# A conv-attention-MoE layer on one core: routing laced into the attention-only steps, with a new step order

## The chip, the core and the metric

The kernel runs on one core of a Trainium2 chip. Five engines work side by side, each through its own list of instructions in order: PE (TensorE, matrix products into PSUM), DVE (VectorE), ACT (ScalarE, functions from tables that must be loaded), POOL (GpSimd) and SP (SyncE, which here only starts DMA transfers). ACT and POOL start transfers too. Engines wait for each other by semaphores. The metric is the device time of one execution in microseconds (us); lower is better.

## The reference

`x` is 16 images of 128 channels and 64 x 64 pixels, thus 4096 tokens each. In float32:

```python
x = x + mamba(group_norm(x))           # state-space scan over tokens, 16 states, 256 inner channels
t = tokens(x)
t = t + causal_attn(layer_norm(t))     # 8 heads, one query vector each; prefix softmax over tokens
t = t + moe(layer_norm(t))
# moe, per image of 4096 tokens:
logits = n @ gate_w.T + gate_b         # 64 experts
probs  = softmax(logits, axis=tokens)
vals, idx = top_k(probs, 8)            # every expert takes its 8 best tokens
pooled = sum_k n[idx] * vals           # one row of 128 per expert
out = gelu(pooled @ w1 + b1) @ w2 + b2
result[token] += out[expert] * vals    # for the tokens that the expert took
```

## The kernel before

**Joint steps.** Every image is cut into 8 blocks of 512 tokens, so there are 128 blocks and the main loop makes one step for each. The scan (mamba) works on block k and the attention on block k - 9. A step has 16 parts n, one for each state. In each, DVE makes a product `bx` (`product`) and two scans of 512 (`scan`); POOL multiplies the result by the broadcast C row (`da`) and PE adds it up into `y_ps`; SP loads the next states' B and C rows as a broadcast from memory (`load_bc`, three n ahead, five buffers); ACT makes the decays (`decay`, an Exp, up to eight n ahead). For n = 1, 3, 5 and 7 a POOL transfer adds a pair of products instead (`add_pair`).

**The order by hand.** All other work is placed by the table `STEP`: for each n three strings, one before the first scan, one between the two scans and one after them. A name in it is an operation: `k0`..`k7` keys, `s0 s1` scores, `v0`..`v7` values, `mx less sexp` score maximum and exponential, `w0 w1` weights from the split scores, `a..` attention products, `d` one decay, `y..` a transpose-add of one state, `lnsc lnap` layer norm, `ge0`..`ge4` the end of the group norm, `ar0`..`ar3` the residual added to a finished image by POOL transfers with addition, `sr0`..`sr3` its store, `spread` the reading back of the split scores, `tu fin` the turn and store of half an attention block. All engines keep this order, and SP, ACT and POOL their transfers in it.

**Attention-only steps.** After the 128th block the scan is over. The loop goes on for ten more steps with the attention's last nine blocks (the tenth is short). DVE and POOL have almost nothing to do there.

**Routing.** A loop of its own follows. A pair of images is handled together (8 pairs, 64 blocks). For every block it loads the channel columns `t` of both images, turns them on PE (`turn`), takes mean and variance on DVE (8 `bn_stats`, 8 `bn_aggr`), makes logits (16 PE records), scales and turns them, normalizes the tokens on ACT (`normed`, 8 activations). Once per pair `choose` finds the 8 largest logits of every expert among 4096, takes Exp and keeps the chosen ones; twelve blocks later `turn_chosen` and `pool_chosen` sum the tokens.

**Experts and final sum.** 16 groups of 4 experts with weights in four buffers, then for every image a product of outputs and chosen probabilities added to `t2_d` and stored.

PSUM is shared by small pools: `ps` has three banks that nearly all PE results pass through.

Of the kernel before, what the change touches and what calls it, by code (L numbers as in the profile page):

```python
# [11 lines left out]
ALU = mybir.AluOpType  # L12
# [27 lines left out]
def conv_attn_hybrid(ctx: ExitStack, tc: tile.TileContext, x, w_in, conv_w, conv_b, w_xproj, w_dt, b_dt,  # L40
# [27 lines left out]
    g_d = dram.tile([NB // 2, P, T], F32, name="g_d")  # L68
    o_d = dram.tile([NB, E, O], F32, name="o_d")
# [4 lines left out]
    ones = const.tile([P, P], F32, name="ones")  # L74
    nc.gpsimd.memset(ones, 1.0)
# [6 lines left out]
    with ExitStack() as st:  # L82
# [3 lines left out]
        yps = st.enter_context(tc.tile_pool(name="yps", bufs=1, space=PSUM))  # L86
        bps = st.enter_context(tc.tile_pool(name="bps", bufs=1, space=PSUM))
# [26 lines left out]
        wv = wp.tile([P, HD, P], F32, name="wv")  # L114

# [100 lines left out]

        xp = st.enter_context(tc.tile_pool(name="xp", bufs=1))
        xsp = st.enter_context(tc.tile_pool(name="xsp", bufs=2))
        xbp = st.enter_context(tc.tile_pool(name="xbp", bufs=2))
        mp = st.enter_context(tc.tile_pool(name="mp", bufs=2))  # L220
        m1 = st.enter_context(tc.tile_pool(name="m1", bufs=1))
        dap = st.enter_context(tc.tile_pool(name="dap", bufs=13))
        hp_ = st.enter_context(tc.tile_pool(name="hp", bufs=2))
        bcp = st.enter_context(tc.tile_pool(name="bcp", bufs=5))
        tmp = st.enter_context(tc.tile_pool(name="tmp", bufs=6))
        vp_ = st.enter_context(tc.tile_pool(name="vp", bufs=4))
        a1 = st.enter_context(tc.tile_pool(name="a1", bufs=1))
# [30 lines left out]
        def gn_end(b, part):  # L258
# [11 lines left out]
            if part == 2:  # L270
                DVE.tensor_tensor(gs[:, 1:2], mv[:, 0:1], gs[:, 0:1], ALU.subtract)
                DVE.scalar_tensor_tensor(gs[:, 1:2], gs[:, 1:2], gs[:, 1:2], mv[:, 1:2], ALU.mult, ALU.add)
# [191 lines left out]
        def store_residual(b, part):  # L464
            SP.dma_start(t1_d[b, :, bass.ts(part, T // 4)], res[b][:, bass.ts(part, T // 4)])
# [236 lines left out]
        def take_o(m):  # L702
            s = att[m]
            s["ot"] = short("ot")
            ACT.copy(s["ot"][:, : 2 * P], s.pop("o")[:, :2, :].rearrange("p q d -> p (q d)"))

        def turn_o(m, f):
            s = att[m]
            s["to"] = bank("to_ps")
            ot = s.pop("ot")  # L710
            for q in range(2):
                PE.transpose(s["to"][:, bass.ts(q, P)], ot[:, bass.ts(q, P)], ident)

        def finish(m, f):
            b, i = divmod(m, NBLK)
            s = att[m] if f == 0 else att.pop(m)
            xs = short("tx")
            ACT.copy(xs[:, : 2 * P], s.pop("to")[:, : 2 * P])
            ACT.dma_start(t2_d[b, :, i * L + f * (L // 2) : i * L + (f + 1) * (L // 2)], xs[:, : 2 * P])

# [4 lines left out]
            ("lx0 k0 k4 yp14", "yp15", "takey k1 k2"),  # L725
            ("k3 v6", "norm skip", "tu0 fin0"),
            ("", "k5", "ge0 s0 k6 turny ge1 k7"),
            ("s1", "gate0", ""),
            ("v4 v7 ge2 gate1 v5 mx d d y-1 conv0", "d less y1", "sexp"),
            ("w1 a10 a11 exp d ts1", "ge3 outp d put tsc ssp c1 d", ""),  # L730
            ("", "", "conv1"),
            ("ar0 ssum ar1 b1 d slog rest1 ar2 split1 y3 to1 rest2 d conv2 csilu", "split2", "d store v0"),
            ("tu1 lx1 v2 ge4", "fin1 cen", ""),
            ("", "", ""),
            ("v1 xproj v3 z delta sq exp bcs", "var", "lnsc"),
            ("", "y5 y7", "spread inv w0 d"),
            ("gnl a00 a01", "y8", "d y9 lb ar3 sr0"),
            ("sr1 d y10 y11 ts0 d", "c0 y12", ""),
            ("b0", "", "sr2"),
            ("d lnap gns", "du", "nt d d sr3 y13 d d to0"),  # L740
# [37 lines left out]

        for k in range(NK + LAG + 1):
            b, i = divmod(k, NBLK)  # L780
            cur = k if k < NK else None
# [37 lines left out]
            for f in range(2):  # L819
                ops[f"tu{f}"] = (mp_, lambda m, f=f: turn_o(m, f))  # L820
                ops[f"fin{f}"] = (mp_, lambda m, f=f: finish(m, f))
# [9 lines left out]
            def do(n, part):  # L831
                for name in STEP[n][part].split():
                    if name == "d":
                        decays(k, n, 1)
                        continue
                    of, f = ops[name]
                    if of is not None:
                        f(of)

# [19 lines left out]
    ff = ctx.enter_context(tc.tile_pool(name="ff", bufs=1))  # L859
    pooled = ff.tile([P, E, 32], F32, name="pooled")  # L860
    nc.gpsimd.memset(pooled, 0.0)
    with ExitStack() as st:
        PE, DVE, ACT, POOL, SP = (InOrder(tc, e) for e in (nc.tensor, nc.vector, nc.scalar, nc.gpsimd, nc.sync))
        NG = CB * 2
        LATE = 12
        AHEAD = 5
        xps = st.enter_context(tc.tile_pool(name="rxps", bufs=2, space=PSUM))
        lps = st.enter_context(tc.tile_pool(name="rlps", bufs=1, space=PSUM))
        sps = st.enter_context(tc.tile_pool(name="rsps", bufs=1, space=PSUM))
        acc = st.enter_context(tc.tile_pool(name="racc", bufs=1, space=PSUM))  # L870
        big = st.enter_context(tc.tile_pool(name="big", bufs=2))
        tsp = st.enter_context(tc.tile_pool(name="tsp", bufs=12))
        xnp = st.enter_context(tc.tile_pool(name="xnp", bufs=LATE + 3))
        rp_ = st.enter_context(tc.tile_pool(name="rp", bufs=2))

        def bank():
            return sps.tile([P, CB, P], F32, tag="s", name="s_ps")

        cmat = rp_.tile([P, P], F32, name="cmat2", bufs=1)
        DVE.tensor_tensor(cmat, ident, mean_w, ALU.subtract)  # L880
        gn = rp_.tile([E, C], F32, name="gn", bufs=1)
        SP.dma_start(gn, gate_w)
        gb = rp_.tile([P, 1], F32, name="gb", bufs=1)
        for j in range(2):
            SP.dma_start(gb[j * E : (j + 1) * E, :], gate_b.unsqueeze(1))
        gt_ps = bank()
        PE.transpose(gt_ps[:, 0, :E], gn, ident[:E, :E])
        gt = rp_.tile([P, E], F32, name="gt", bufs=1)
        DVE.tensor_copy(gt, gt_ps[:, 0, :E])
        gc_ps = bank()  # L890
        PE.matmul(gc_ps[:, 0, :E], cmat, gt, start=True, stop=True)
        gtc = rp_.tile([P, E], F32, name="gtc", bufs=1)
        DVE.tensor_copy(gtc, gc_ps[:, 0, :E])
        tc.keep_in_program_order(nc.scalar.preload_act_table_set(EXP_LN))

        NIT = NB // 2 * NBLK
        blk, pair = {}, {}

        def load_tokens(it):
            p, i = divmod(it, NBLK)  # L900
            w = blk[it] = {}
            w["t"] = [tsp.tile([P, L], F32, tag="t", name="t") for _ in range(2)]
            for j in range(2):
                SP.dma_start(w["t"][j], t2_d[2 * p + j, :, bass.ts(i, L)])

        def turn(it):
            w = blk[it]
            w["x"] = xps.tile([P, CB, 2, P], F32, tag="x", name="x_ps")
            for c in range(CB):
                for j in range(2):  # L910
                    PE.transpose(w["x"][:, c, j, :], w["t"][j][:, bass.ts(c, P)], ident)

        def logits(it):
            w = blk[it]
            w["l"] = lps.tile([P, NG, E], F32, tag="l", name="l_ps")
            for c in range(CB):
                for j in range(2):
                    PE.matmul(w["l"][:, 2 * c + j, :], w["t"][j][:, bass.ts(c, P)], gtc, start=True, stop=True)
            w.pop("t")

        def stats(it):
            w = blk[it]
            s6 = rp_.tile([P, NG, 6], F32, tag="s6", name="s6")
            mv = w["mv"] = rp_.tile([P, NG, 2], F32, tag="mv2", name="mv2")
            for g in range(NG):
                DVE.bn_stats(s6[:, g, :], w["x"][:, g // 2, g % 2, :])
            for g in range(NG):
                DVE.bn_aggr(mv[:, g, :], s6[:, g, :])

        def scales(it):  # L930
            w = blk[it]
            mv = w["mv"]
            rs = w["rs"] = rp_.tile([P, NG], F32, tag="rs", name="rs", bufs=3)
            ACT.activation(rs, mv[:, :, 1], AF.Ln, bias=eps)
            ACT.activation(rs, rs, AF.Exp, scale=-0.5)

        def shifts(it):
            w = blk[it]
            nm = w["nm"] = rp_.tile([P, NG], F32, tag="nm", name="nm", bufs=3)
# [207 lines left out]
```

## Time and profile before

| what | us |
|---|---|
| median of 3 runs (lowest to highest) | 9916.12 (9912.14 to 9921.84) |
| profiled execution | 9941.12 |
| its span | 9939.4 |
| joint steps (0 to about 8690) | 8690 |
| attention-only steps (about 8690 to 9102) | 412 |
| routing (9102 to 9573) | 471 |
| experts (9573 to 9712) | 139 |
| final sum (9712 to the end) | 227 |

Over the span PE is busy 86%, DVE 88%, ACT 74% and POOL 73%; DMA moves 1783 MB at a mean of 179 GB/s. These are averages over stages with different limits, so the stages are read apart. Mean durations that matter: `bx` 1280 ns, a scan 1267 ns, a table load 1283 ns, Exp over 4096 columns 3760 ns, `bn_stats` of 128 283 ns, `match_replace` of 4096 4409 ns, a half of the chosen probabilities 2330 ns. A busy PE is not PE at its peak, since its instructions overlap.

### The profile page before, as it was taken

How to read it: one execution, taken by the hardware profiler on the slowest of the kernel's cores; microseconds unless marked ns; L12 is line 12 of the kernel's file. 1: busy time of each engine (PE TensorE's matmuls, PEld its weight loads, DVE VectorE, ACT ScalarE, POOL GpSimd, SP SyncE). 2: the span in 40 equal slices, each digit the busy share in tenths (PEclk: the TensorE clock that was granted, in tenths of full speed). 3: DMA queues.
4: the chain of work that ended last, by engine and by line, in shares of the span. 5: the costliest groups of instructions: out<-in, count | busy, mean ns of one | idle time of the engine just before them, and what ended most of it. 6: DMA issues, size and time to landing. Idle time of an engine off the chain costs nothing.

```text
span 9939.4 us, 183919 instructions
## 1 busy us (share of the span) xinstructions
PE 8516.5 (86%) x69084; PEld 5113.5 (51%) x69084; DVE 8709.0 (88%) x9217; ACT 7385.9 (74%) x14079; POOL 7301.8 (73%) x4475
## 2 busy tenths in 40 slices
PE   5579898998989898989999898989898998877775
PEld 3345555555555555555555555555555555545642
DVE  8999999999999999999999999999999999902743
ACT  4568787888878887878878788878788887755730
POOL 7888888888888888888888888888888888800000
PEclk7789999999999999999999999999999999998976
DMA  6677777777776777777777777777777777611358
GB/s 164 173 188 181 189 185 190 183 179 192 181 194 176 197 181 189 182 191 180 186 190 177 194 181 193 180 194 178 194 181 192 183 178 186 163 38 55 119 169 352
DMA packets 978014, 1783.42 MB, mean 179 GB/s; under 512 B 194953, under 2 KB 275489, under 8 KB 967905
## 3 DMA queue, kind: packets, MB, share of 16 engines
q1 hardware_dynamic: 724480, 1381.32, 50.1%
q0 software_dynamic: 82944, 302.03, 15.4%
q10 hardware_dynamic: 169696, 88.30, 3.1%
q8 instruction: 544, 8.91, 0.3%
q14 instruction: 350, 2.86, 0.1%
HBM read 1363.99 MB, written 138.94 MB: 151 GB/s over the span
## 4 chain that ended last, share of the span: by engine, by line
PE 45%; ACT 34%; DVE 9%; DMA 6%; issue 5%; ACTq 1%; SPq 0%; POOL 0%; DVEq 0%; POOLq 0%
ACT da L31 11%; PE ao_ps L31 9%; PE v_ps L31 9%; PE y_ps L31 6%; ACT L31 6%; PE k_ps L31 4%; DVE h L31 3%; DVE bx L31 3%; PE o_ps L31 2%; PE z_ps L31 2%; ACT xc L31 2%; PE xs_ps L31 2%; PE var_ps L31 2%; ACT kt L31 2%; DMA bct<-bcs 2%
## 5 line engine op out<-in xcount | busy, mean ns | idle before, releaser
L31 POOL TENSOR_TENSOR da<-h,bct 128x1024 f32<-128x1024 f32 x2048 | 6626.3, 3240 | 1275.8 <-DVE h L31 667.0
L31 DVE TENSOR_TENSOR_SCAN h<-da,state,bx 128x512 f32<-128x512 f32 x3584 | 4420.8, 1267 | 201.6 <-DVE bx L31 4.3
L31 DVE TENSOR_TENSOR bx<-du,bct 128x1024 f32<-128x1024 f32 x2048 | 2621.4, 1280 | 115.0 <-DMA bct<-bcs 45.8
L31 ACT ACTIVATE da<-delta,a_neg 128x512 f32<-128x512 f32 x4096 | 2621.8, 714 | 27.9 <-DMA da<-da 17.2
L31 PE MATMUL y_ps<-ident,da 128*128 128x128 f32 x12288 | 1708.5, 296 | 236.6 <-POOL da L31 124.5
L31 PEld LDWEIGHTS y_ps<-ident,da 128*128 128x128 f32 x12288 | 1559.7, 154 | 540.8 <-issue 256.3
L31 PE MATMUL v_ps<-wv,xn 128*64 128x512 f32 x4096 | 1074.6, 624 | 200.3 <-ACT xc L31 134.9
L31 ACT ACTIVATE v<-v_ps 128x512 f32<-128x512 f32 x1024 | 610.8, 598 | 790.6 <-PE v_ps L31 790.0
L31 PE MATMUL k_ps<-xn,wk 128*128 128x512 f32 x2048 | 1038.7, 613 | 97.6 <-ACT kt L31 93.1
L31 PE MATMUL xs_ps<-xb,wc 128*128 128x512 f32 x2048 | 975.7, 609 | 23.7 <-ACT xt L31 4.2
L31 ACT ACTIVATE kt<-k_ps 128x512 f32<-128x512 f32 x1024 | 565.6, 612 | 234.2 <-PE k_ps L31 165.0
L31 PE MATMUL ao_ps<-v,wm 128*64 128x128 f32 x8192 | 580.4, 286 | 151.9 <-ACT wm L31 150.7
L31 ACT ACT_TABLE_LOAD x526 | 674.9, 1283 | 14.1 <-ACT parts L31 4.4
L31 DVE TENSOR_TENSOR_SCAN h<-da,bx 128x512 f32<-128x512 f32 x512 | 600.8, 1208 | 32.5 <-POOL state L31 3.0
L31 PEld LDWEIGHTS v_ps<-wv,xn 128*64 128x64 f32 x4096 | 228.5, 137 | 745.6 <-ACT xc L31 232.4
L31 PEld LDWEIGHTS ao_ps<-v,wm 128*64 128x64 f32 x8192 | 453.8, 140 | 267.4 <-ACT wm L31 213.5
L31 PEld LDWEIGHTS xs_ps<-xb,wc 128*128 128x128 f32 x2048 | 366.0, 193 | 368.8 <-issue 321.7
L31 POOL DMA_DIRECT2D da<-da x512 | 460.0, 899 | 98.4 <-POOL state L31 65.4
L31 PEld LDWEIGHTS k_ps<-xn,wk 128*128 128x128 f32 x2048 | 331.2, 190 | 349.4 <-ACT kt L31 215.6
L31 PE MATMUL var_ps<-sq,mean_w 128*128 128x512 f32 x256 | 219.6, 953 | 277.8 <-ACT sq L31 277.8
L31 POOL COPY state<-h 128x2 f32<-128x2 f32 x1792 | 432.4, 241 | 0.0
L31 PEld LDWEIGHTS s_ps<-kt,q 128*32 128x32 f32 x16384 | 257.2, 110 | 271.6 <-issue 97.8
(209 smaller groups left out, 10326.6 us busy)
## 6 DMA issues: line engine op xcount, KB each, us to landing
bct<-bcs SPq DMA_DIRECT2D x2048, 512.0 KB
da<-da POOLq DMA_DIRECT2D x512, 512.0 KB, 7.9
xs<-t_d SPq DMA_DIRECT2D x240, 256.0 KB
xs<-in_x_dram SPq DMA_DIRECT2D x128, 256.0 KB
t_d<-xt SPq DMA_DIRECT2D x64, 512.0 KB
t_d<-tx ACTq DMA_DIRECT2D x256, 128.0 KB
t<-t_d SPq DMA_DIRECT2D x128, 256.0 KB
tc<-t_d SPq DMA_DIRECT2D x16, 2048.0 KB
```

The source lines that it names most:

```text
L31: return lambda *args, **kw: self.tc.keep_in_program_order(f(*args, **kw))
```

## The change

- Routing becomes a class whose instructions are put into the attention-only steps. A step has 48 slots (16 n times three parts); `plan` gives every call a slot, `at` makes the calls of a slot after the step's own work. It begins with the second attention-only step. Slots 0 to 431 exist. Blocks 0 to 55 (seven pairs) are planned to be pooled; what lies past slot 431 and the eighth pair follow in `rest`.
- For it the attention stores its result twice: as channel columns (`t2_d`, as before) and as token rows (`t2t`), 128 KB at a time on SP (`st0 st1`). Statistics and pooling read these rows, four rows of 512 B (2 KB) per partition, on SP and on POOL's queue.
- Routing itself changes: no turning of x; variance from the two halves of `bn_stats`; logits with experts as rows, scaled by 1/std that goes through memory (`rs_d`) and comes back as a broadcast; the gate's bias enters only into Exp; the chosen probabilities are multiplied by 1/std of their token, the mean is taken off the pooled row, and the division by the denominator moves to the pooled row and to the experts' outputs (`rden`).
- A new table `STEP` for all steps. The residual's four parts are added at n = 6, 8, 9 and 10, and their stores move from SP to ACT.
- In the group norm, the difference of means goes through PSUM (`far`).
- Expert weights: five buffers, loads four groups ahead, the first four before `rest`.
- The gate's weights are prepared at the start; the scan's pools lie on the right side and are closed before the lacing begins.

```diff
@@ gn_end
             if part == 2:
-                DVE.tensor_tensor(gs[:, 1:2], mv[:, 0:1], gs[:, 0:1], ALU.subtract)
-                DVE.scalar_tensor_tensor(gs[:, 1:2], gs[:, 1:2], gs[:, 1:2], mv[:, 1:2], ALU.mult, ALU.add)
+                far = w["gp"][:, 1:2]
+                DVE.tensor_tensor(far, mv[:, 0:1], w["gp"][:, 0:1], ALU.subtract)
+                DVE.scalar_tensor_tensor(gs[:, 1:2], far, far, mv[:, 1:2], ALU.mult, ALU.add)
@@ store_residual
-            SP.dma_start(t1_d[b, :, bass.ts(part, T // 4)], res[b][:, bass.ts(part, T // 4)])
+            ACT.dma_start(t1_d[b, :, bass.ts(part, T // 4)], res[b][:, bass.ts(part, T // 4)])
@@ take_o, store_tokens
-            s["ot"] = short("ot")
...
+            s["ot"] = op_.tile([P, 2 * P], F32, tag="ot", name="ot")
...
+        def store_tokens(m, f):
+            b, i = divmod(m, NBLK)
+            at = i * L + f * (L // 2)
+            SP.dma_start(t2t_d[b // 2][b % 2, at : at + L // 2, :].rearrange("(q p) c -> p q c", p=P),
+                         att[m].pop("ot").rearrange("p (q c) -> p q c", c=C))
@@ class routing
+            def load_rows(self, it, name, pool, queue):
+                p, i = divmod(it, NBLK)
+                x = self.w[name, it] = pool.tile([P, 2, CB, C], F32, tag=name, name=name)
+                for j in range(2):
+                    queue.dma_start(x[:, j], t2t_d[p][j, bass.ts(i, L), :].rearrange("(p r) d -> p r d", r=CB))
...
+                for g in range(8):
+                    DVE.bn_stats(self.pair[p]["s6"][:, 8 * i + g, :], x[:, g // CB, g % CB, :])
...
+            def load_scales(self, it):
...
+                rb = self.w["rb", it] = self.rb.tile([P, CB, P], F32, tag="rb", name="rb")
+                for j in range(2):
+                    SP.dma_start(rb[j * E : (j + 1) * E].rearrange("p r t -> p (r t)"),
+                                 rs_d[p, i, bass.ts(j, L)].partition_broadcast(E))
...
+                l = self.w["l", it] = self.lps.tile([P, L], F32, tag="l", name="l_ps")
+                t = self.w.pop(("t", it))
+                for j in range(2):
+                    PE.matmul(l[j * E : (j + 1) * E, :], gtc, t[j], start=True, stop=True)
...
+                ACT.activation(w["g"], w["lg"], AF.Exp, bias=w["neg"], accum_out=w["den"])
...
+                DVE.match_replace(out=w["lg"], in_to_replace=w["top"], in_values=w["lg"], imm_value=NEG)
...
+                DVE.scalar_tensor_tensor(g, lg, NEG, g, ALU.is_equal, ALU.mult)
+                SP.dma_start(g_d[p, :, cols], g)
...
+        ROUTE = dict(b=42, keep=6, logit=0, lsc=2, llo=-10, d=108, turn=0, scale=6, pool=12, lxd=2, center=15, turnp=18, keepp=21,
+                     stats=(-7, -4, 8, 20, 23, 26, 29, 30), first=(5, 8, 11, 14, 17, 20, 23, 26), last=28, lst=-6,
+                     spread=(32, 35, 38, 41), choose=(95, 98, 101, 104, 107))
@@ STEP
-            ("lx0 k0 k4 yp14", "yp15", "takey k1 k2"),
-            ("k3 v6", "norm skip", "tu0 fin0"),
-            ("", "k5", "ge0 s0 k6 turny ge1 k7"),
-            ("s1", "gate0", ""),
-            ("v4 v7 ge2 gate1 v5 mx d d y-1 conv0", "d less y1", "sexp"),
-            ("w1 a10 a11 exp d ts1", "ge3 outp d put tsc ssp c1 d", ""),
-            ("", "", "conv1"),
-            ("ar0 ssum ar1 b1 d slog rest1 ar2 split1 y3 to1 rest2 d conv2 csilu", "split2", "d store v0"),
-            ("tu1 lx1 v2 ge4", "fin1 cen", ""),
-            ("", "", ""),
-            ("v1 xproj v3 z delta sq exp bcs", "var", "lnsc"),
-            ("", "y5 y7", "spread inv w0 d"),
-            ("gnl a00 a01", "y8", "d y9 lb ar3 sr0"),
-            ("sr1 d y10 y11 ts0 d", "c0 y12", ""),
-            ("b0", "", "sr2"),
-            ("d lnap gns", "du", "nt d d sr3 y13 d d to0"),
+            ("lx0 k0 ge0 yp14 k4", "yp15", "takey k1 k2"),
+            ("k3 v6", "ge1", ""),
+            ("", "", "tu0 s0 skip k5 fin0 k6 turny k7 y-1 d norm s1 v4"),
+            ("", "gate0", ""),
+            ("v7 gate1 mx v5 d w1 d", "less d sexp ge2", ""),
+            ("exp conv0 d y1 a10 ge3 a11", "tsc lx1 outp ts1", "put st0"),
+            ("ssp", "", "c1 ar0"),
+            ("conv1 ssum d d slog rest1 split1 rest2 conv2 d y3", "", "b1 csilu"),
+            ("split2 to1 store tu1 fin1 v0", "v2", "ar1"),
+            ("d", "", "ar2"),
+            ("cen z v3 v1 xproj delta sq var exp bcs", "ge4 d", "ar3"),
+            ("st1", "spread y5 y7 lnsc", ""),
+            ("", "y8 inv w0", "gnl lb d y9 d y10 a00 a01 sr0"),
+            ("y11 ts0 nt d", "", "sr1"),
+            ("c0", "b0", "sr2"),
+            ("d d lnap y12 to0 gns d d", "d du", "y13 sr3"),
@@ main loop
+            if k == NK + 1:
+                mamba.close()
+                ff = ctx.enter_context(tc.tile_pool(name="ff", bufs=1, side="right", reuse_waits="tile"))
+                late = ctx.enter_context(ExitStack())
+                route = routing(late)
...
+                if route is not None:
+                    route.at(((k - NK - 1) * N + n) * 3 + part)
@@ experts
+    WAHEAD = 4
+    for e0 in range(0, WAHEAD * EG, EG):
+        load_weights(e0)
+    route.rest()
...
+            if e0 + WAHEAD * EG < E:
+                load_weights(e0 + WAHEAD * EG)
@@ final sum
+            nc.vector.tensor_scalar(on, on, rden[:, pr : pr + 1], None, ALU.mult)
```

## The prediction, made before the result

> **What bounds the kernel now.** I read first the engine shares in 40 slices, then the busy time per stretch. The columns are: stretch, length, busy time and instruction count of PE, PEld, DVE, ACT and POOL, then clock, DMA share and GB/s.
>
> ```profile
> 5596.00:5662.00 66.00, 59.55 (x506) 35.21 (x502) 63.17 (x60) 54.56 (x103) 56.34 (x37) 0.97 0.70 184
> 8743.00:9095.00 352.00, 287.42 (x2842) 153.82 (x2840) 16.99 (x63) 205.83 (x433) 0.00 (x0) 0.91 0.08 21
> 9102.00:9573.00 471.00, 362.04 (x3085) 319.29 (x3083) 334.09 (x1260) 313.96 (x794) 0.09 (x1) 0.88 0.34 111
> 9573.00:9712.00 139.00, 103.50 (x960) 39.47 (x960) 15.73 (x32) 10.84 (x17) 0.00 (x0) 0.64 0.80 238
> 9712.00:9940.00 228.00, 127.63 (x256) 55.69 (x256) 83.02 (x128) 0.00 (x0) 0.00 (x0) 0.66 0.90 370
> ```
>
> One row per stage: a joint step (scan and attention) is held by DVE at 96%; the attention-only steps use PE and ACT and leave DVE, POOL and 92% of the DMA free; routing has no engine over 77%; the experts and the final sum lean on DMA. So 352 us of idle DVE and DMA stand right before 471 us that need them.
>
> The starts of the score maximum, one per step, give a joint step as 66.0 us (1198.44 to 1264.44), and the same in most others; the step that follows an image's end takes 72 to 76, and the one with the group norm's end 69. An attention-only step takes (9059.0 - 8751.4)/7 = 43.9. Around one image's end, the timelines of POOL and DVE and the waits of SP show why:
>
> ```profile
> 7094.86 2.66 POOL L31 DMA_DIRECT2D xt<-in_x_dram  x3 [0.89 <-ACT xt L31]
> ```
> ```profile
> 7097.84 3.17 DVE L31 TENSOR_TENSOR bx<-du,bct 128x1024 f32<-128x1024 f32 x1
> ...
> 7103.52 4.27 DVE L31 TENSOR_TENSOR bx<-du,bct 128x1024 f32<-128x1024 f32 x1
> ...
> 7133.17 1.52 DVE L31 TENSOR_TENSOR bx<-du,bct 128x1024 f32<-128x1024 f32 x1 [2.16 <-DMA bct<-bcs]
> ```
> ```profile
> SPq L31 <- DMA xt<-in_x_dram: 12.8, 1, 12.8
> ```
>
> Three residual transfers in a row make POOL late, and the products on DVE (1.23 us elsewhere) stretch to 3.17 and 4.27. Later SP waits 12.8 us for the last of them, and the broadcast load behind it is 2.16 us late for DVE. That is 5.0 + 2.7 us of this end's 8.3 (74.35 - 66.0).
>
> ACT and PE are nearly as full. In the chain of waits over 5600 to 5760 no DVE item appears; it runs PE and ACT in turn:
>
> ```profile
> 5664.98 0.60 ACT v L31
> 5665.59 1.28 ACT L31
> 5666.89 3.79 ACT da L31 x6
> 5670.67 0.24 ACT w L31 x2
> 5670.91 0.49 ACT wm L31
> ```
>
> The 1.28 is a table load between Silu and Exp. So DVE's 66.0 and the ACT/PE round (66.1 here) are a near tie.
>
> **What the Trainium skill says.** "SBUF — State Buffer", section "Who interferes with whom": a DVE instruction with two SBUF inputs contends with a GpSimd instruction that reads SBUF, the later one blocked in full. The trace agrees: the group-norm subtraction takes 0.16 us with POOL idle and 2.32 under it.
>
> ```profile
> L31 DVE TENSOR_TENSOR gs<-mv,gs x16: 160/2322/2327, 29.0 to 8025.5; 128x1 f32<-128x1 f32 x16
> ```
>
> "ScalarE: Activation LUTs", section "What ACT_TABLE_LOAD costs": 1283 ns for a load plus a 1380 ns drain. The trace agrees on 1283; of the drain nothing shows (load at 5665.59, next Exp at 5666.89), so I price 1.28. "DMA: Bandwidth & Descriptors", section "Issuing engines are not separate DMA queues": SP, ACT and POOL transfers share the same 16 engines. So row loads on POOL save SP issue time but no transfer time; no run here separates the two yet.
>
> **Part by part, joint loop (0 to 8690).** Subtraction with one operand in PSUM: 15 x (2.32 - 0.16) = -32. Residual transfers at n = 6, 8, 9, 10 in place of three at n = 7 and one at n = 12; their stores move from SP to ACT. The SP wait goes: -2.7 per image. The burst's 5.0: pair additions at n = 5 and 7 stand beside the four, so POOL still issues six transfers (0.88 each) within six n; I take half, -2.5 (between 0 and -5.0). 15 x 5.2 = -78. ACT now waits if a store comes before its residual has landed; the last is issued at n = 10 and stored at n = 14, some 15 us for a landing of 12.8: nothing, or up to 3 us of ACT per image, covered by decays eight n ahead.
>
> Token stores: 256 of 128 KB on SP at n = 5 and 11, 33.6 MB over a DMA at 0.73; their source is copied 3 or more n earlier, so SP should not stand. Zero; +30 if the broadcast loads, queued behind on SP, come later. Loads of weights and gate moved to the start: below 5 us.
>
> New order: I counted the functions on ACT. A decay (Exp) now sits at n = 2 between key 7 and value 4 (both Silu): two more loads, 2 x 1.28 = 2.57 us of ACT per step. ACT has 11 us idle per step, and value 4 waits there now anyway (2.19 us for PE); PE has y-1, score 1 and value 4 to do meanwhile. One decay fewer then stands before the weights' Exp (-1.26), and w1 comes before the others. I take +0.3 per step, 128 x 0.3 = +38; ends: -0.5 (waits shortened elsewhere) and +2.57. Loop: -32 - 78 + 38 = -72.
>
> **Attention-only steps.** The first of nine is unlaced. Slots 0 to 383 fall in the eight full steps from 8743 (351.5 us), 384 to 431 in the short last step (7 us now). By the slots, 57 blocks get logits and 44 are pooled in the eight steps. PE per block: logits are two 64-wide, 512-long matmuls, the form of the values (four records in 1.08): 0.95; four transposes 0.5; eight pooling matmuls 1.0 (16 records 1.09 today). 57 x 0.95 + 44 x 1.5 = 120. The eight transposes of x and four of logits, 8 Identity activations and 8 aggregations per block disappear. Exp of 4096 columns lands at n = 0 among the keys: 3.76 + 0.24 + two loads 2.57 = 6.6, six times, 39, all on the ACT/PE round. DVE per block: statistics 1.7, scaling 0.7 and 0.7, half a maximum 0.6, and (4.4 + 2 x 2.33 + small)/8 = 1.2: 39 us in a full step, which fits 70, but stands in line ahead of the score maximum: with DMA waits 3 us in each of 6 full steps, 18. PE idles 352 - 287 = 65 us there; routing fills perhaps 26. Sum 351.5 + 120 + 39 + 18 - 26 = 502, a full step being about 70.
>
> Short step: choice of pair 6 (4.0 beside 4.4, then 4.7) and eight pooled blocks: 30. The rest: 8.4 MB of expert weights are ahead on SP of the last rows and logits (238/0.80 = 298 GB/s at full share: 28 us, over four pooled blocks); then statistics, scales, their way through memory, two logit blocks, about 13; choice 9; eight blocks at 1.7, 14: 65. Thus 8743 + 502 + 30 + 65 = 9340 in place of 9573: -233.
>
> Experts: four of 16 groups are loaded; twelve, 25 MB, take 84 us at that rate, PE's own work is 103.5: 108 for 139, -31. Final sum: eight small multiplications, +2; its DMA bound stays.
>
> Total -72 - 233 - 31 + 2 = -334. The profiled execution took 9941.1 us, so 9607; the median of the runs is 25 lower (9916.1): 9582.
>
> **Rivals.**
> - DMA and SP bind the laced steps. Per block 0.52 MB each of statistics rows, pooling rows and channel columns, 0.26 broadcast scales, 0.26 chosen: 2.1 MB; at 111/0.34 = 326 GB/s 6.4 us, a full step 52 + 4. Below 70, but single-buffered scales and one in-order queue that also carries attention's small loads could stretch a step to 85: +90, 9672. For: eight blocks arrive unevenly. Against: 30% slack.
> - All goes well: image ends vanish (15 x 8.3), PE gaps filled twice as well: loop -155, tail -295: 9466. Against: the ACT/PE round at 66.1 to 66.6 takes over.
> - Slower: the table loads. If ACT/PE has no room, 2.57 us is added to each of 119 steps with attention, +306, and the image ends and group norm save nothing as DVE no longer sets the pace; with the tail's -262, +44: 9960. It decides from about 2.2 us per step. For: the chain above never leaves ACT and PE. Against: ACT idles at that place already.
> - Lacing displaces instead of overlapping, PE stalling on each DVE answer: steps of 95 us, +150, 9732.
>
> **How the numbers follow.** Chances: forecast 0.55 (own range 9500 to 9660), DMA 0.15, all well 0.12, displaced 0.05, table loads 0.10, a mixture near no change 0.03. Range 9470 to 9740 leaves out mainly the last two and a little beyond. Faster by over 0.2% (20 us, about what a measurement of this kernel tells from nothing) 0.87, within 0.03, slower 0.10.
>
> **What would show it.** Joint steps at 66.0 to 66.5 and image ends at 70; subtraction under 0.3 us; two more table loads per step with no new PE wait before value 4; laced steps near 70 with DMA share about 0.75; last pooled block near 9270 (loop's -72 included); experts near 108. A joint step above 68, or DVE waiting on scale loads in most blocks, would prove me wrong.

## The result and the profile after

The kernel after took 10017.12 us (median of 4 runs, 10005.61 to 10023.94), the kernel before, run beside it, 9918.98 (9912.14 to 9924.85). The ratio is 1.0098 (95% interval 1.0081 to 1.0116): slower by 1%, where I had forecast 9582. Both profiled executions lie above those medians: 10023.94 for after, with a span of 10021.1, and 9941.12 for before.

The spans divide as follows. A "mark" is the start of the score maximum in step k; the first step of the kernel is k = 9.

| stretch | before, us | after, us | change | predicted |
|---|---|---|---|---|
| start to the mark of k = 127 | 8636.9 | 8842.8 | +206 | -72 |
| from there to the experts | 936.7 | 832.4 | -104 | -233 |
| experts | 138.4 | 121.8 | -17 | -31 |
| final sum | 227.4 | 224.1 | -3 | +2 |
| whole span | 9939.4 | 10021.1 | +82 | -334 |

The busy time per stretch of the kernel after, one row per stage (a joint step, six laced steps and more, what follows the last mark, the experts, the final sum); the columns are those of the prediction's table:

```profile
5791.10:5859.38 68.28, 60.76 (x508) 36.95 (x509) 63.73 (x60) 57.38 (x106) 56.64 (x37) 0.95 0.71 183
8958.20:9489.50 531.30, 397.89 (x3459) 212.14 (x3461) 279.34 (x734) 224.29 (x416) 40.48 (x76) 0.86 0.66 208
9489.50:9675.20 185.70, 106.66 (x869) 66.11 (x871) 71.63 (x120) 36.33 (x63) 26.19 (x48) 0.76 0.70 221
9675.20:9797.00 121.80, 94.94 (x961) 35.37 (x962) 16.01 (x33) 10.84 (x17) 0.00 (x0) 0.84 0.71 219
9797.00:10021.00 224.00, 134.96 (x256) 58.58 (x256) 84.12 (x135) 0.00 (x0) 0.00 (x0) 0.64 0.89 364
```

In the first row DVE is busy 63.73 us, much as before (63.17), but the step is 68.28 long: DVE has gone from 96% to 93% and no longer sets the pace. ACT's busy time rose from 54.56 to 57.38, which is the decay's two loads and little else. Averaged over the loop, by the kind of step (89 plain ones, 15 at the place where the group norm of the next image ends, 14 with an image's end; the last of the 15 belongs to the last image, which has no next one):

| kernel | plain | group norm | image end |
|---|---|---|---|
| before | 66.35 | 69.11 | 74.26 |
| after | 68.09 | 69.42 | 78.01 |

89 x 1.74 + 15 x 0.31 + 14 x 3.75 = 155 + 5 + 53 = 212 us, which is the loop's loss but for a start that is 6 us earlier. The granted TensorE clock over these steps is 0.96 before and 0.95 after, but PE's busy time per step is 60.85 and 60.95 us, so a slower PE is not where the time goes.

Where a plain step loses it is seen on ACT's timeline. Columns: start, duration, engine, line, operation, tiles, count, and in brackets the idle time before. First the kernel before, key 7 (`kt`), value 4 (`v`) and the copy of the output product (`xt`):

```profile
5660.47 0.60 ACT L31 ACTIVATE kt<-k_ps 128x512 f32<-128x512 f32 x1 [1.22 <-PE k_ps L31]
5663.26 0.60 ACT L31 ACTIVATE v<-v_ps 128x512 f32<-128x512 f32 x1 [2.19 <-PE v_ps L31]
...
5676.66 1.05 ACT L31 COPY xt<-o_ps 128x512 f32<-128x512 f32 x1 [0.39 <-PE o_ps L31]
```

Then the kernel after, the same place and what follows:

```profile
5789.17 0.60 ACT L31 ACTIVATE kt<-k_ps 128x512 f32<-128x512 f32 x1 [1.22 <-PE k_ps L31]
5789.78 1.28 ACT L31 ACT_TABLE_LOAD   x1
5791.08 1.33 ACT L31 ACTIVATE da<-delta,a_neg 128x512 f32<-128x512 f32 x2
5792.32 0.80 ACT L31 ACTIVATE xb<-xb,gs 128x515 f32<-128x515 f32 x1
5793.14 1.28 ACT L31 ACT_TABLE_LOAD   x1
5794.43 1.57 ACT L31 ACTIVATE v<-v_ps 128x512 f32<-128x512 f32 x3
...
5806.37 1.04 ACT L31 COPY xt<-o_ps 128x512 f32<-128x512 f32 x1 [1.10 <-PE o_ps L31]
```

Before, ACT idles 2.19 us in front of value 4, value 4 starts 2.79 after key 7 and `xt` 16.19 after it. After, the gap holds a load, the decay, the norm (`xb`) and a load back: value 4 starts 5.26 and `xt` 17.20 after key 7. PE meanwhile, in the kernel before:

```profile
5662.13 2.80 PE L31 MATMUL v_ps<-wv,xn 128*64 128x512 f32 x12
5664.86 1.09 PE L31 MATMUL y_ps<-ident,xc 128*128 128x128 f32 x8
5665.79 3.60 PE L31 MATMUL xs_ps<-xb,wc 128*128 128x512 f32 x8
```

And in the kernel after:

```profile
5790.96 2.80 PE L31 MATMUL v_ps<-wv,xn 128*64 128x512 f32 x12
5795.08 0.87 PE L31 MATMUL w_ps<-rh,lh 94*128 94x256 bf16 x4 [1.32 <-ACT v L31]
```

PE has finished the three values and stands 1.32 us until ACT has read one of them and its bank is free. In this order nothing else is placed there for PE: `y-1` and the first convolution, which before has behind value 5 (`y_ps<-ident,xc` and `xs_ps` above), were moved ahead of value 4 and behind w1.

An image's end still has a burst of POOL transfers, now at other n. On DVE in the kernel after:

```profile
5595.06 2.25 DVE L31 TENSOR_TENSOR bx<-du,bct 128x1024 f32<-128x1024 f32 x1
5599.81 5.22 DVE L31 TENSOR_TENSOR bx<-du,bct 128x1024 f32<-128x1024 f32 x1
```

And the table loads between 655 and 8600 us (count, busy total, mean ns, idle time before them and what ended most of it), first of before:

```profile
L31 ACT ACT_TABLE_LOAD x469 | 601.7, 1283 | 8.5
L235 ACT ACT_TABLE_LOAD x235 | 301.5, 1283 | 4.2
```

Then of after:

```profile
L31 ACT ACT_TABLE_LOAD x685 | 878.9, 1283 | 37.8 <-DMA t_d<-xt 25.8
L250 ACT ACT_TABLE_LOAD x229 | 293.8, 1283 | 4.1
```

914 loads, against 469 + 235 = 704 before; by the steps that this stretch holds, 7.9 per step for 5.9. The 25.8 us behind `t_d<-xt` are ACT standing at its own residual stores, 1.7 per image.

In the full laced steps the marks lie 84.9, 79.3, 81.6, 82.0 and 81.4 us apart. The waits of three of them, 9165.27 to 9408.06, first DVE's, PE's and SP's own (total, times, longest):

```profile
DVE lg L31 <- DMA rb<-rs_d: 42.8, 17, 6.4
DVE lg L31 <- ACT g L31: 27.1, 3, 9.2
...
PE l_ps L31 <- DVE lg L31: 39.3, 10, 8.4
...
SPq L31 <- DVE g L31: 53.4, 3, 17.9
```

DVE waits for the broadcast scales in 17 of the 24 blocks, 14 us per step, and 9 per step in front of the match-and-replace until ACT has taken Exp of the pair; behind that, SP waits 18 with the store of the chosen probabilities, and all its later loads with it. PE's wait for `lg` is in part the same delay handed on: in e6 below, which moves the choice, it is 16.6.

### The profile page after: what moved, and what is told of

Read it like the earlier page. It is cut to its first block, busy times and chain, and to the rows that moved or that the text cites. A ratio compares the mean times of both kernels' runs of the same rounds, so it can differ in the third digit from the quotient of the medians.

```text
span 10021.1 us, 180411 instructions
## 1 busy us (share of the span) xinstructions
PE 8383.7 (84%) x67557; PEld 5023.0 (50%) x67557; DVE 8703.6 (87%) x8781; ACT 7446.0 (74%) x13569; POOL 7369.7 (74%) x4602
## 5 line engine op out<-in xcount | busy, mean ns | idle before, releaser
L31 ACT ACTIVATE da<-delta,a_neg 128x512 f32<-128x512 f32 x4096 | 2659.4, 715 | 144.2 <-DMA rh<-pd 83.8
L31 PEld LDWEIGHTS y_ps<-ident,da 128*128 128x128 f32 x12288 | 1620.5, 158 | 642.1 <-issue 403.5
L31 PE MATMUL y_ps<-ident,da 128*128 128x128 f32 x12288 | 1755.7, 300 | 201.6 <-POOL da L31 102.4
L31 PE MATMUL k_ps<-xn,wk 128*128 128x512 f32 x2048 | 1070.3, 627 | 119.5 <-ACT kt L31 109.0
L31 ACT ACT_TABLE_LOAD x774 | 993.0, 1283 | 44.3 <-DMA t_d<-xt 25.8
L31 PE MATMUL v_ps<-wv,xn 128*64 128x512 f32 x4096 | 1007.3, 611 | 18.8 <-DVE gs L31 18.5
L31 ACT ACTIVATE v<-v_ps 128x512 f32<-128x512 f32 x1024 | 585.8, 597 | 288.2 <-PE v_ps L31 286.7
L31 POOL DMA_DIRECT2D xd<-t2t_d x128 | 70.2, 585 | 676.8 <-PE pl_ps L31 656.0
L31 PE MATMUL var_ps<-sq,mean_w 128*128 128x512 f32 x256 | 242.5, 1046 | 277.8 <-ACT sq L31 277.8
```

The costliest lines, as they stand in the source:

```text
L31: return lambda *args, **kw: self.tc.keep_in_program_order(f(*args, **kw))
```

## The experiments

Fifteen kernels in six groups. Ratios are to the kernel before, with their 95% intervals; the kernel after stands at 1.0098. Steps are given as plain / group norm / image end.

**1. Which part of the new step costs.** e1 takes the one decay out of the gap and puts it behind value 5:

```
-  "tu0 s0 skip k5 fin0 k6 turny k7 y-1 d norm s1 v4"
-  "v7 gate1 mx v5 d w1 d"
+  "tu0 s0 skip k5 fin0 k6 turny k7 y-1 norm s1 v4"
+  "v7 gate1 mx v5 d d w1 d"
```

> The changed kernel with one edit: the decay that stands between key 7 and value 4 (n = 2) goes back behind value 5 (n = 4), so the two table loads per step go. Theory T (the two loads lengthen the ACT/PE round): joint steps fall from 68.3 to 66.4-66.9 us, the whole to about 9815 us (118 steps x 1.7 less). Rival O (the rest of the order, above all the late turn of y and the wait for it in DVE, holds the round): joint steps stay above 67.8, the whole within 30 us of 10017. Attention-only steps: the same 80-82 us laced under both.

9813.9 us, 0.9889 (0.9874 to 0.9904); steps 66.86 / 67.51 / 73.67; 704 loads again. Moving one pair of Exp back is worth 203 us: 1.23 per plain step, 1.9 per group norm, and 4.3 per image end.

e1 also shows what the spread of the residual transfers does when ACT and PE are on time. The products at an image's end no longer stretch: together they exceed their usual 1.23 us by 0.75 per end, against 6.5 in before and in after. But DVE now waits 7.8 us per end for the broadcast loads (3.0 in before). One end of e1:

```profile
5502.19 1.23 DVE L31 TENSOR_TENSOR bx<-du,bct 128x1024 f32<-128x1024 f32 x1 [2.35 <-DMA bct<-bcs]
...
5511.40 1.23 DVE L31 TENSOR_TENSOR bx<-du,bct 128x1024 f32<-128x1024 f32 x1 [5.51 <-DMA bct<-bcs]
```

SP issues these loads in order. Among them it no longer waits for the residual itself (12.4 us per end in before), but 9.7 for a residual store of ACT to land, and 12.7 in place of 6.1 for the split scores (`pd<-parts`).

e2 keeps all of the change but the step's order and the residual's schedule: the table `STEP` of before, with `st0` at n = 5 and `st1` at n = 11, and the residual stores on SP.

> The changed kernel with the step order of before (token stores put in at n = 5 and n = 11) and the residual stores back on SP; lacing, token stores and PSUM difference stay. T and O both: joint steps about 66.3, image ends 72-76, whole about 9790. Rival D (the added 33.6 MB of token stores slow the joint steps): joint steps above 67. The group-norm end step (69.6 now, 69.5 before) should fall by about 2 us if the PSUM difference is worth what the subtraction shows, and not fall if the ACT/PE round holds it.

9791.64, 0.9866 (0.9853 to 0.988); steps 66.52 / 66.93 / 73.48. Order and residual schedule together have nothing to their credit: without them the kernel is 225 us faster than after. Its image ends exceed its plain steps by 7.0; those of e1, with split transfers, by 6.8.

e3 is the kernel before with a decay moved to the same place, between key 7 and value 4:

```
-  "ge0 s0 k6 turny ge1 k7"
-  "v4 v7 ge2 gate1 v5 mx d d y-1 conv0"
+  "ge0 s0 k6 turny ge1 k7 d"
+  "v4 v7 ge2 gate1 v5 mx d y-1 conv0"
```

> The kernel before with one edit: one decay moved from n = 4 to between key 7 and value 4. T: two more table loads per step, joint steps 66.2 -> 67.8-68.6, whole 10100-10200 us. O: joint steps within 0.5 us of before, whole below 9980.

9916.74, 0.9993 (0.9985 to 1.0002); steps 66.29 / 68.90 / 73.63. Its loads, in the joint loop:

```profile
L31 ACT ACT_TABLE_LOAD x704 | 903.2, 1283 | 12.7
L235 ACT ACT_TABLE_LOAD x236 | 302.8, 1283 | 4.2
```

940 loads in place of 704, and no time lost. Value 4 is late here too, 4.56 us after key 7, but `xt` comes 16.00 after it, no later than in before. So a table load has no price by itself here: the same two loads at the same place cost 203 us in the new order and nothing in the old.

**2. What makes the gap overfull.** Beside the decay, the new order differs there in two ways: `norm` stands in the same gap (before has it at n = 1), and PE's `y-1` and first convolution are no longer behind value 5. e9 puts PE's work back, e13 the norm, e14 both; the decay stays in the gap in all three.

```
e9, e14   -  "... k7 y-1 d norm s1 v4"   "v7 gate1 mx v5 d w1 d"             "exp conv0 d y1 a10 ..."
          +  "... k7 d norm s1 v4"       "v7 gate1 mx v5 y-1 conv0 d w1 d"   "exp d y1 a10 ..."
e13, e14  -  "ge1"        "... d norm s1 v4"
          +  "norm ge1"   "... d s1 v4"
```

> The changed kernel with y-1 and conv0 on PE put back behind value 5, ahead of the weights' matmul, as before; the decay with its two table loads stays at n = 2. Theory C (the loads cost only because the new order took from behind the late values the PE work that needs nothing from them, so that PE stands at the weights' matmul for a bank): joint steps fall from 68.1 to 66.4-67.2, the whole to 9830-9890. Rival L (ACT alone is too full with two loads more, wherever PE's work lies): joint steps stay at 67.7 or more, the whole above 9970.

e9: 10013.57, 1.0094 (1.0079 to 1.011); steps 68.25 / 69.28 / 76.85. PE's cover alone changes nothing in the total.

> The kernel after with one edit: the group norm's application (norm, one ACT activation of 0.80 us per step, between key 7's and value 4's Silu in the new order) goes back to n = 1, where before has it. The decay stays at n = 2. Theory G (the gap before value 4 has room for either the decay with its loads or the norm, and both overfill it): a plain step falls from 68.1 to 66.9-67.3, the run to about 9880-9930 (ratio 0.996-1.001). Rival L (the two loads cost their 1.3-1.6 us wherever ACT stands in the new order): plain step within 0.2 of 68.1, run within 15 us of the kernel after (10005-10030).

e13: 9939.26, 1.0015 (1.0006 to 1.0023); steps 67.61 / 68.14 / 77.00. Between both expectations: the norm is a part of it, 0.48 of the step, and neither theory alone has it.

> The kernel after with both differences to e3's cheap arrangement undone at the gap: norm at n = 1, y-1 and the first convolution behind value 5, decay stays between key 7 and value 4. Theory G2 (in e3 the same loads cost nothing because neither norm nor other PE work shares the gap): a plain step of 66.4-67.2, run 9800-9900 (ratio 0.988-0.998). Rival L (the loads cost because of what follows: the rest of the new order gives ACT no idle time before the step's end): plain step above 67.7, run above 9950.

e14: 9841.79, 0.9911 (0.9896 to 0.9925); steps 67.11 / 67.51 / 73.58. Both together give 175 us back with the decay where it was (1.0 per plain step, 1.9 per group norm, 4.4 per image end). ACT of e14:

```profile
5809.16 0.60 ACT L31 ACTIVATE kt<-k_ps 128x512 f32<-128x512 f32 x1 [1.22 <-PE k_ps L31]
5809.78 1.28 ACT L31 ACT_TABLE_LOAD   x1
5811.07 1.34 ACT L31 ACTIVATE da<-delta,a_neg 128x512 f32<-128x512 f32 x2
5812.43 1.28 ACT L31 ACT_TABLE_LOAD   x1
5813.72 1.57 ACT L31 ACTIVATE v<-v_ps 128x512 f32<-128x512 f32 x3
...
5825.13 1.05 ACT L31 COPY xt<-o_ps 128x512 f32<-128x512 f32 x1
```

And PE of e14 at the same place:

```profile
5810.82 2.80 PE L31 MATMUL v_ps<-wv,xn 128*64 128x512 f32 x12
5813.55 1.09 PE L31 MATMUL y_ps<-ident,xc 128*128 128x128 f32 x8
5814.48 3.60 PE L31 MATMUL xs_ps<-xb,wc 128*128 128x512 f32 x8
5817.92 0.60 PE L31 MATMUL w_ps<-rh,lh 94*128 94x256 bf16 x4
```

Value 4 is still late, 4.56 us after key 7, but PE goes from the values to `y-1` and the convolution without a gap, and when w1 comes its bank has long been read. The 1.32 us of PE are gone, and so are the 1.10 that ACT then stood before `xt`. From key 7 to `xt` e14 takes 15.97 us, after 17.20, e13 16.50, e1 15.62. Against e1 0.25 per plain step remains, for the decay's place and PE's together. e9 has most of this stretch too (16.67). Where it loses it again shows when the intervals between marks are sorted by their place in the image. In the new order `ge2` to `ge4` come after the mark, so the group norm's end reaches into the interval behind, which the averages above count as plain. With these two intervals taken together, and what is left called ordinary:

| kernel | ordinary step (76) | two steps of the group norm's end (14 pairs) | image end (14) |
|---|---|---|---|
| before | 66.41 | 135.34 | 74.26 |
| e3 | 66.33 | 135.16 | 73.63 |
| e2 | 66.41 | 134.07 | 73.48 |
| after | 68.09 | 137.57 | 78.01 |
| e1 | 66.33 | 137.30 | 73.67 |
| e9 | 67.79 | 140.12 | 76.85 |
| e13 | 67.42 | 136.85 | 77.00 |
| e14 | 66.57 | 137.57 | 73.58 |

In an ordinary step the decay's place costs 1.76 us in the new order (after against e1), and the rest of the order nothing (e1 against before). The cover alone gives back 0.30 of it, the norm alone 0.67, both 1.52: more than the sum. e9 gains 0.30 in each ordinary step and loses 2.55 per image at the group norm. There PE stands, in the new order, until the group norm's `gs` is ready: per image 2.2 us at a weight load of the values and 1.7 at one of `o_ps` in e9 and e14, 1.9 at the latter alone in e1, and not at all in e2. These waits point to the placement of `ge2` and `ge3` as a cost of its own, 3.2 us per image between e1 and e2; no run here moves it alone.

**3. The residual's stores.** e4 is after with the four stores per image on SP in place of ACT, one word of the diff (`ACT.dma_start` to `SP.dma_start` in `store_residual`).

> The changed kernel with the residual stores back on SP. Theory A (at an image's end ACT stands behind the stores, which wait for the residual's landing: 6.2 + 2.3 us seen at one end): image-end steps fall from 77.7 to about 74, whole by 45-60 us. Rival B (the burst of POOL transfers and its block of DVE is the cost; SP's wait takes ACT's place): image ends stay at 76-78, whole within 15 us.

9948.13, 1.0024 (1.0014 to 1.0034); steps 67.82 / 69.32 / 75.13. The stores on ACT cost 69 us, 2.9 of it at each image end, when ACT is already late. In e1 they stand on ACT too and the ends take 73.67, so they cost where ACT has nothing to spare.

**4. The subtraction.** e12 is the kernel before with this one edit (`far` in PSUM).

> The kernel before with the group norm's difference in PSUM and nothing else. Theory: the subtraction falls from 2.32 to below 0.3 us and the group-norm step from 69.1 to about 67, the whole by 30 us. Rival: the ACT/PE round holds that step, and it stays at 69.

9906.76, 0.9986 (0.9979 to 0.9992); steps 66.49 / 66.92 / 73.81. The operation in e12:

```profile
L31 DVE TENSOR_TENSOR gn_ps<-mv,gn_ps x16: 155/156/165, 29.1 to 7995.6; 128x1 f32<-128x1 f32 x16
```

2322 ns became 156, and the step with it loses 2.19 us. This agrees with the Trainium skill, "SBUF — State Buffer", section "Who interferes with whom": a DVE instruction with two SBUF inputs contends with a GpSimd instruction that reads SBUF. The edit puts the result into PSUM as well as one input, so which of the two counts is not separated. 15 x 2.19 = 33 us by the steps, but 14 by the medians (8 to 21 by the interval). The steps of before come from an execution that is 20 us above its median, those of e12 from one 3 above, and e12's plain steps came out 0.14 longer; so 33 is the less certain of the two.

**5. The laced steps.** e5 and e6 change after: e5 gives the broadcast scales a second buffer (in memory that is free by then) and loads them two slots earlier; e6 chooses earlier, `choose=(91, 92, 101, 104, 107)` for `(95, 98, 101, 104, 107)`: the pair's maximum and its Exp move from the end and the first keys of the next step to n = 14 of their own step.

> The changed kernel with a second buffer for the broadcast scales (in the space of the residual tile, which is free by then) and their load two slots earlier, so that a load does not wait for the scaling of the block before. Theory R (this one buffer makes a chain of scaling, load, scaling, and PE's logits wait behind it): laced steps fall from 81.5 to 70-74 us, the whole from 10017 to 9940-9965. Rival Q (SP's one queue and the DMA's load bring everything late alike): laced steps stay at 79-82, the whole within 15 us of 10017.

e5: 10010.5, 1.0089 (1.0075 to 1.0102); laced steps 77.6 to 81.8. Over the five full laced steps DVE's wait for the scales falls from 67.9 to 31.8 us, that for the statistics' rows rises from 28.7 to 44.2, and that for `g` stays at 45.

> The changed kernel with the choice of a pair and its Exp at slots 91 and 92 in place of 95 and 98, so Exp stands among the decay's and weights' Exp at the end of a step and not among the keys. Theory X (two table loads per pair and a maximum on DVE that waits up to 9 us for this Exp sit on the laced step): laced steps 4-6 us shorter, the whole by 25-35 us. Rival: the wait is hidden behind the scales' chain; within 10 us of 10017.

e6: 9966.55, 1.0046 (1.0032 to 1.0059); laced steps 71.7 to 75.5. Over its three steps from 9131.58:

```profile
9131.58:9353.28 221.70, 181.04 (x1646) 101.15 (x1648) 137.45 (x351) 91.30 (x174) 25.53 (x48) 0.90 0.80 253
```

Seven us per step in these three, 8.7 over the five full ones (the traced execution is e6's fastest, 28 us below its median, so the lower figure is the safer one): the wait of DVE for `g` is gone, SP's behind it falls from 53.4 to 24.5, and two loads per step go from ACT (99.0 busy to 91.3). The DMA share is now 0.80. DVE's wait for the scales is untouched (42.4).

e11 is e2 with the early choice, e7 with that and the second buffer.

> The kernel of e7 with one buffer for the broadcast scales again. If the second buffer is worth nothing here too (as in e5): within 8 us of 9711; if it counts once the early choice has made room: 9730-9760.

> The kernel of e2 (old order, stores on SP) with both edits, second buffer and early choice. If R and X hold and add up: laced steps 66-70 us in place of 82, the whole 9690-9715 us, from 9792. If Q holds: 9760 or more.

e11: 9738.31, 0.9811 (0.9797 to 0.9824), laced steps 73.4 to 75.9. e7: 9710.51, 0.9789 (0.9776 to 0.9802), laced steps 70.8 to 75.2. By these medians the buffer that gave 7 us alone, within the noise, gives 28 once the choice is out of its way. In the traces the difference is smaller: from the mark of k = 128 to the experts the buffer takes 770.6 to 757.6 us alone (after, e5) and 726.2 to 704.1 behind the early choice (e11, e7); in e5's total part of this is hidden by a joint loop 9 us longer. e7 is the fastest complete kernel of this study: 208 us below before, 307 below after.

e10 and e15 start from e7. e10 loads statistics' rows and logits' columns for even blocks only, so that a quarter of the routing's bytes and the issues that go with them are gone; e15 loads all of the statistics' rows, but on POOL's queue instead of SP's.

> The kernel of e7 with the statistics' rows and the logits' columns loaded for even blocks only; odd blocks are computed from the even block's data, so a quarter of routing's bytes and four of its some six SP issues per two blocks are left out. If transfers or SP's queue set the laced steps: from 72.5 to 60-64. If PE, ACT and their order set them: 70-72.5. My own sum without any wait for DMA gives 66.

> The best kernel so far (old step, second buffer for the scales, early choice: 9710.5, laced step 72.5) with one edit: the statistics' token rows are loaded on POOL's queue in place of SP's; the bytes are the same. If SP's queue of issues and waits sets the laced step: 63-68 us per laced step, run 9640-9690. If the transfers themselves set it (DMA busy 0.81): laced steps within 2 us of 72.5, run within 20 us of 9710. If POOL's issue adds a delay of its own: laced steps above 75, run above 9730.

e10: 9642.64 (a single execution), laced steps 59.6 to 63.6. e15: 9727.24, 0.9792 (0.9775 to 0.9808), laced steps 70.2 to 76.5. Three laced steps by the busy time per stretch, first of e7:

```profile
8909.00:9127.54 218.54, 177.89 (x1646) 96.54 (x1648) 137.18 (x352) 90.50 (x174) 25.54 (x48) 0.90 0.80 256
```

Of e10:

```profile
8877.35:9066.08 188.73, 170.50 (x1646) 94.92 (x1648) 136.68 (x352) 90.14 (x174) 25.54 (x48) 0.96 0.71 222
```

Of e15:

```profile
8915.42:9140.78 225.36, 177.91 (x1646) 97.44 (x1648) 137.59 (x352) 90.48 (x174) 54.06 (x102) 0.89 0.77 247
```

Fewer transfers take 30 us from three steps, with the same number of instructions on PE, DVE and ACT. Over the five full laced steps DVE's waits for scales and rows fall from 81 to 31 us, 10 per step of the 10.9 that a step gains. So with the choice moved, a laced step waits on its loads. Whether it is their bytes, the latency of each in a chain of loads, or SP's issues e10 does not tell, since it takes all of these away; at 0.80 the DMA isn't full. The granted clock is also higher in e10 (0.96 for 0.90) and PE busy 7.4 us less in these three steps, which can be a part of the 30 or a consequence.

Another queue for the same bytes takes nothing and adds 7 in these three steps (0.8 per step over the five), while POOL's busy time doubles. The Trainium skill, "DMA: Bandwidth & Descriptors", section "Issuing engines are not separate DMA queues", says that transfers from all these engines run on the same 16 DMA engines and that a second issuer saves only issue time; the rate here, 247 for 256 GB/s, agrees. That SP's queue is free of blame e15 does not show: DVE's waits for scales and rows fall by 21 us in the three steps, but PE's wait for the split scores (`rh<-pd`), which SP still loads, rises from 13.7 to 32.0.

**6. The last rows.** e8 is e7 with the last pair's rows and columns loaded ahead of the experts' weights.

> The kernel of e7 with the last rows and logits of the eighth pair loaded before the first 8.4 MB of expert weights and not behind them. The wait of the statistics for them was 28.6 us in the changed kernel: if it is on the path, another 20-28 us less than e7; if the eighth pair waits for PE or the earlier pair anyway, within 8 us of e7.

9713.99, 0.9789 (0.9776 to 0.9803). In the kernel after, between the last mark and the experts, the wait that it removes:

```profile
DVE s L31 <- DMA xa<-t2t_d: 28.6, 1, 28.6
```

In e7 it is 23.6 at its longest, in e8 it is gone, and the stretch is 6 us shorter (178.2 to 171.9). In its place DVE now waits 18.6 us for the broadcast scales of the last blocks, whose loads still stand behind the weights on SP. The weights come later for it: e8's experts and final sum take 342 where e7's take 329. A wait of 24 us was worth 6 where it stood and nothing at the end.

## Why the prediction was wrong

**The step that failed: the new order.** "I take +0.3 per step, 128 x 0.3 = +38." Measured: +1.74 per plain step. In an ordinary step all of the loss is the decay between key 7 and value 4: 1.76 between after and e1, which is back at before's time. With its share in the other steps the decay is 203 us. The rest of the order costs some 3 us per image, at the group norm (e1 against e2), a term that I did not have. I counted the instructions rightly (two more loads per step, 5.9 to 7.9; the load 1283 ns) and the idle time rightly (2.19), and set them against each other as if nothing else used that time. The order moved three things, and I priced only the first: the decay into the gap, the norm into the same gap, and PE's work away from behind the values. I wrote that PE would have "y-1, score 1 and value 4 to do meanwhile"; all of these come before the values' banks are full, and the wait is after. What the gap has to hold is 1.28 + 1.33 + 0.80 + 1.28 = 4.7 us against 2.2 of idle time. The other 2.5 make value 4 late; PE then stands 1.32 us, and `xt` is 1.0 later than before. That the overfull gap and the missing PE work do this together e14 shows: with both put back, the decay may stay at a cost of 0.24 per ordinary step.

**The rival that came true in part.** The slower rival said "2.57 us is added to each of 119 steps": as a price of the loads alone it is refuted by e3. Its condition, no room on ACT and PE, is what happened. With +1.74 per plain step the joint loop stayed short of the 2.2 from which I had it decide; the kernel is slower all the same, because the tail brought 124 us and not 262. That this rival's 9960 lies nearest is thus partly luck: its price per load was wrong.

**Residual transfers, -78.** Spreading them gave nothing that can be seen in the time: the image ends exceed the plain steps by 6.8 in e1 (spread) and 7.0 in e2 (not spread), by 7.9 in before. Of its two terms, the burst was taken too low where the rest is on time: in e1 nearly all of the stretch is gone (6.5 to 0.75 per end), in after, where the engines are late, none of it. The other, "The SP wait goes: -2.7 per image", had the wait wrong: SP waits for the stores and the split scores instead, and DVE's wait for the broadcast loads rises from 3.0 to 7.8, which takes back what the burst gave. "nothing, or up to 3 us of ACT per image" for the stores was the right bound, 2.9 in e4; but the cover, decays eight n ahead, was not there, since ACT had become the late engine, and I took the end at nothing.

**Subtraction, -32.** Right in its mechanism: 156 ns. Its size is 33 us by the steps of e12 and 14 by the medians. In the kernel after it brings nothing: the two steps of the group norm's end take 137.57 against 135.34, with the decay's loss and PE's wait for `gs` in them.

**Token stores, 0.** Right: plain steps take 66.52 in e2, which has them, and 66.49 in e12, which hasn't.

**Laced steps, +150 and a full step of about 70.** The eight intervals from the mark of k = 128 grew from 361 to 585 us, by 224. The +150 was for the eight full steps, and most of the last of them lies behind the last mark, so the miss here is at least 74. I had named the single buffer and SP's one queue in the rival at 85 and thought 30% of slack enough. Two terms were missing from the sum: the choice as planned makes DVE, then SP, wait for an Exp among ACT's keys (7 to 9 us per step, e6), and the waits for loads, of which e10 takes away 10 per step by leaving out a quarter of the bytes. I had priced the throughput of the transfers, 52 of 70, and not these waits; what in them is bytes, latency or issue stays open.

**The rest, 65.** The wait for rows behind the weights was 28.6 where I worked out 28. Yet the stretch from the last mark to the experts fell short by the rest of routing's 129 us, some 55 at most, and e8 shows that the wait was not what was to be gained: the scales' way back through memory was next. What else the stretch lost stays open. The experts gained 17 of 31, the final sum was right.

**Total.** -334 became +82: 278 of the miss in the loop, 129 in the attention-only steps and routing, 14 in the experts, -5 in the final sum.

## What to carry to other kernels

Idle time of an engine can be spent once. When an order is rewritten, write down for each gap everything that lands in it on that engine, and for the engine on the other side what it has to do until the gap's end; edits that are harmless one at a time (e3) can overfill it together. And when work is laced into steps that have room by throughput, look for the longest hand-over between engines and for loads that others wait for: here moving one hand-over gave 7 to 9 us per step (e6), before any buffer was added.

## What the runs showed of the hardware

- A load of ACT's table takes 1283 ns wherever it stands, but two more per step cost nothing in e3 (66.33 us per ordinary step for 66.41) and 1.76 us per ordinary step in after (against e1), where a norm of 0.80 us stood in the same gap and PE had no other work behind it.
- A product on DVE that takes 1.23 us took 2.25 and 5.22 in after beside POOL's issues of transfers, which were themselves 1.65 to 3.28 us there in place of 0.88: both are stretched. In e1 the same spread issues, 0.86 to 0.89 us each, stood beside products of 1.23. So an issue alone does not do it; POOL's own products run between them, and which overlap stretches the two was not separated.
- Moving 2 KB-row loads from SP's to POOL's queue changed the DMA's rate from 256 to 247 GB/s and the laced step from 72.5 to 73.4 us (five steps each): no gain from a second issuing engine.
